# A two-layer attention and mixture-of-experts kernel: who evicts the projections of the first attention, and where three small steps stand in its order

## The chip, the cores and the metric

The kernel runs on one core of one Trainium2 chip. The metric is the device time of one execution in microseconds (us), of which the median of several runs is given. Every engine of the core has a queue of its own and works through it in order: TensorE multiplies, VectorE and ScalarE read its results from PSUM, GpSimd works on SBUF alone, and SyncE issues most loads. Inputs are single-precision floats throughout.

## The reference

Two layers, each an attention with a residual and a mixture of experts with a residual. Only the first attention is touched by the change. There the 1024 tokens of each of two batches are normalised twice and serve as keys and values, together with 77 context tokens; the queries are taken from the tokens too:

```python
xn = _layernorm(x, ln1_w, ln1_b)          # here: the context, 77 tokens
latn = _layernorm(latents, ln2_w, ln2_b)  # here: the normalised tokens, 1024
q = latn @ Wq                             # 16 heads of 64
k, v = jnp.split(jnp.concatenate([xn, latn], axis=1) @ Wkv, 2, axis=-1)
weight = softmax(einsum('bhld,bhnd->bhln', q * scale, k * scale))
out = einsum('bhln,bhnd->bhld', weight, v) ... @ Wo
```

After it come a top-2 router with eight experts of width 1024, a second attention on the 77 context tokens, and a second mixture with a causal convolution.

## The kernel before

**Units.** The first attention is cut into 32 units. A unit is a pair of heads (line names: `j` is 0 or 1) and half of the queries, 512 of them, in four tiles of 128; there are 2 batches, 8 pairs and 2 halves. Four units share one group of four heads (`G`), whose weights are loaded together. A unit goes through these steps:

- `score` (L697): for a tile `t` of queries, the scores against 1024 token keys for both heads, into two PSUM tiles `sc` of their own. VectorE takes the negated maximum of each (L707), ScalarE the exponential with that maximum as bias and the sum as a by-product (L708), which gives the probabilities `pa`.
- `context_scores` (L672 to L687): the same for the 77 context keys, for all four tiles at once; `sums_context` (L690) adds these up on VectorE.
- `join` and `combine` (L715 to L735): the two parts of the softmax are brought to one maximum, the factors `f` are worked out on VectorE in small steps, and `pa` is scaled by them: by GpSimd (L731), and in the last unit half by VectorE (L735) and half by ScalarE (L733). `scale_context` (L739) does it for the context part.
- `turn_tile` (L749): TensorE transposes the scaled probabilities, four blocks of 128 keys into one PSUM tile, for head 0 and then head 1; head 0 is evicted to `pT` by ScalarE (L117), head 1 by VectorE (L121). `k0` is 0 or 4, the first or second half of the keys. `turn_context` (L762) does it for the context part, with ScalarE.
- `attend` (L774): the product of `pT` with the values, 9 tiles of keys, into one PSUM tile `po`; its result is evicted to `oT`, and `out_part` (L642, L650) multiplies that by the output weights and lets VectorE add it to the residual.

**Projections.** Queries and keys of a pair come from `qk_part` in five pieces (L627), values of a group from `v_part` in five pieces (L603). Their products, the transposes, the output products and the routing steps all take their PSUM tiles from one pool of three buffers with the tag "t". A new product or transpose can start only when one of the three has been evicted; the scheduler picks which.

**Who evicts.** `evac` (L108 to L123) takes the engine in `to`. Without it a counter `turn` decides: odd calls go to ScalarE, even ones to VectorE. `v_part`, `qk_part`, the context's transposes and the `attend` results are evicted without `to`.

**Order.** Within the attention the order of each engine's queue is the order of the calls (`manual_schedule`). The loop over the units interleaves three of them: in unit `u`, `score` of `u`, `turn_tile` of the unit before (`prev`), and `attend` of `prev` and of the unit before that. Each unit has four turns `t`. A turn first transposes tile `t` of `prev` with `k0` 0, then scores tile `t`, then does the projections that a table `fill[(u, t)]` has for it, then transposes tile `t` with `k0` 4. `plan` spreads the pieces over turns 0, 1, 1, 2, 2 of a unit. In groups of four units this gives: in unit 0 five pieces of queries and keys; in unit 1 four output products; in units 2 and 3 five of queries and keys and five of values. Routing steps of finished tokens and two layer norms are filled in as well, in units 2 to 4 and 18 to 27, and the second attention's context side in units 30 and 31 (`side_context`, `side_keys`, `side_values`). At turn 3 stand `join`, `combine` and `turn_context`.

After the loop the last unit's transposes and `attend` follow, mixed with the output products and the routing of the third block of tokens. Then comes the expert stage, whose weights SyncE's queue loads (L1063, L1068) once the memory of the attention is free.

Of the kernel before, what the change touches and what calls it, by code (L numbers as in the profile page):

```python
# [10 lines left out]
AF = mybir.ActivationFunctionType  # L11
# [6 lines left out]
B, S, D = 2, 1024, 256  # L18
C = 77
# [30 lines left out]
def tile_two_layers(ctx: ExitStack, tc: tile.TileContext, a: dict, out: bass.AP):  # L50
    nc = tc.nc
# [58 lines left out]
    def evac(dst, src, scale=None, to=None):  # L110

        if to is None:
            turn[0] += 1
            to = nc.scalar if turn[0] % 2 else nc.vector
        if to is nc.scalar:
            if scale is None:
                nc.scalar.copy(dst, src)  # L117
            else:
                nc.scalar.activation(dst, src, AF.Copy, scale=scale)
        elif scale is None:  # L120
            nc.vector.tensor_copy(dst, src)  # L121
        else:
            nc.vector.tensor_scalar_mul(dst, src, scale)  # L123
# [73 lines left out]
    bk1 = mat(const, "L1_xattn_bk", [P, 2], "bk1")  # L197
# [242 lines left out]
    def side_context():  # L440
        ctxT = side["ctxT"] = lnp.tile([P, 2, B, C], F32, tag="ctxT", name="ctxT")
        for b in range(B):
            pt = ps_t.tile([P, 512], F32, tag="t", name="pt")
            for c in range(2):
                nc.tensor.transpose(pt[:, c * C : (c + 1) * C], ctx_sb[:, b, c * P : (c + 1) * P], ident[:C, :C])
            evac(ctxT[:, :, b, :], pt[:, : 2 * C].rearrange("p (c s) -> p c s", c=2))

    def side_keys():
        kT = side["kT"] = lnp.tile([P, 2, B * C], F32, tag="kT1", name="kT1")
        ps = ps_t.tile([P, 512], F32, tag="t", name="pk")  # L450
        for c in range(2):
            for ci in range(2):
                nc.tensor.matmul(
                    ps[:, c * B * C : (c + 1) * B * C],
                    w1a["k"][:, ci, c * P : (c + 1) * P],
                    side["ctxT"][:, ci, :, :].rearrange("p b s -> p (b s)"),
                    start=(ci == 0),
                    stop=(ci == 1),
                )
        for c in range(2):  # L460
            nc.scalar.activation(
                kT[:, c, :], ps[:, c * B * C : (c + 1) * B * C], AF.Identity, bias=bk1[:, c : c + 1]
            )

    def side_values():
        v1 = side["v1"] = lnp.tile([C, B, D], F32, tag="ch", name="v1")
# [48 lines left out]
    NG, GC = 4, H0 * DH0 // 4  # L515
    with ExitStack() as st:
# [76 lines left out]
        def v_part(G, k2):  # L593
            b = G // NG
            if k2 == 0:
                v_of[G] = pj.tile([P, NKT, GC], F32, tag="v", name=f"v_{G}")
            v = v_of[G]
            ps = ps_t.tile([P, 512], F32, tag="t", name="pv")
            kts = [kt for kt in (k2, k2 + 1) if kt < NKT]
            for n, kt in enumerate(kts):  # L600
                r = krows(kt)
                for c in range(2):
                    nc.tensor.matmul(  # L603
                        ps[:r, n * GC : (n + 1) * GC],
                        kvT[b][:, c, kt * P : kt * P + r],
                        groups[G]["v"][:, c, :],
                        start=(c == 0),
                        stop=(c == 1),
                    )
            r = krows(k2)  # L610
            evac(v[:r, k2 : k2 + len(kts), :].rearrange("p n f -> p (n f)"), ps[:r, : len(kts) * GC])

        QK = (("q", 0, 512), ("k", 0, 512), ("k", 512, 1024), ("k", 1024, NKEY), ("q", 512, 1024))

        def qk_part(pair, n):
            G, p = pair // 2, pair % 2
            b = G // NG
            if n == 0:
                qk_of[pair] = (
                    pj.tile([P, S], F32, tag="qT", name="qT"),  # L620
                    pj.tile([P, NKEY], F32, tag="kT", name="kT"),
                )
            nm, n0, n1 = QK[n]
            dst = qk_of[pair][nm == "k"]
            ps = ps_t.tile([P, 512], F32, tag="t", name="pqk")
            for c in range(2):
                nc.tensor.matmul(  # L627
                    ps[:, : n1 - n0],
                    groups[G][nm][:, c, p * P : (p + 1) * P],
                    kvT[b][:, c, n0:n1],  # L630
                    start=(c == 0),
                    stop=(c == 1),
                )
            evac(dst[:, n0:n1], ps[:, : n1 - n0], scale=0.125 if nm == "q" else None)

        def out_part(G, t2):
            b = G // NG
# [51 lines left out]
        def sums_context(U):  # L689
            nc.vector.tensor_reduce(U.l[:, 1, :], U.pB.rearrange("p j t s -> p (j t) s"), AX.X, ALU.add)  # L690
# [28 lines left out]
        def combine(U, last=False):  # L719

            m = U.m
            nc.vector.tensor_tensor(U.l, U.l, U.f, ALU.mult)
            nc.vector.tensor_tensor(m, U.l[:, 0, :], U.l[:, 1, :], ALU.add)
            nc.vector.reciprocal(m, m)
            nc.vector.tensor_tensor(U.f, U.f, m.unsqueeze(1).to_broadcast([P, 2, 8]), ALU.mult)
            for t in range(4):
                for j in range(2):
                    r = 4 * j + t
                    pa, f = U.pa[t][:, j, :], U.f[:, 0, r : r + 1]
                    if not last:  # L730
                        nc.gpsimd.tensor_scalar_mul(pa, pa, f)  # L731
                    elif j:
                        nc.scalar.activation(pa, pa, AF.Copy, scale=f)  # L733
                    else:
                        nc.vector.tensor_scalar_mul(pa, pa, f)  # L735
# [5 lines left out]
        def turn_tile(U, t, k0):  # L741

            if t == 0 and k0 == 0:
                U.pT = [ptp.tile([P, NKT, 512], F32, tag=f"pT{j}", name=f"pT{j}") for j in range(2)]
            for j in range(2):
                ps = ps_t.tile([P, 512], F32, tag="t", name="ptr")
                for n in range(4):
                    kt = k0 + n
                    nc.tensor.transpose(  # L749
                        ps[:, n * P : (n + 1) * P], U.pa[t][:, j, kt * P : (kt + 1) * P], ident  # L750
                    )
                evac(
                    U.pT[j][:, k0 : k0 + 4, t * P : (t + 1) * P],
                    ps.rearrange("p (n q) -> p n q", n=4),
                    to=(nc.scalar, nc.vector)[j],
                )

        def turn_context(U):
# [27 lines left out]
        NPAIR, NU = 2 * B * NG, 4 * B * NG  # L786
        routes = [route(blk) for blk in range(NBLK)]
        with tc.manual_schedule(engines=ORDERED):
# [14 lines left out]
            c = contexts()  # L803
# [27 lines left out]
            for n in range(2):  # L831
                m, s, v, t = latents(2 + n)
# [4 lines left out]
                r = routes[n]  # L837
                u = 18 + n
# [18 lines left out]
            prev = None  # L857
            for u in range(NU):
                U = begin(u)
                if u % 4 == 0 and u // 4 + 1 < B * NG:  # L860
                    groups[u // 4 + 1] = load_group(u // 4 + 1)
                for t in range(4):
                    if prev is not None and t > 0:
                        turn_tile(prev, t, 0)
                    score(U, t)
                    if prev is None and t == 0:
                        context_scores(U)
                    if prev is not None:
                        if t == 0:
                            context_scores(U)  # L870
                            if prev.before is not None:
                                attend(prev.before, range(3, NKT))
                                prev.before = None
                            turn_tile(prev, t, 0)
                            turn_tile(prev, t, 4)
                            scale_context(prev)
                        if t == 3:
                            attend(prev, range(3))
                    if t == 1:
                        sums_context(U)  # L880
                    if t == 3:
                        join(U)
                        for it in late.pop(u, []):
                            it()
                        combine(U, u == NU - 1)
                        if prev is not None:
                            turn_context(prev)
                    for it in fill.pop((u, t), []):
                        it()
                    if prev is not None and t > 0:  # L890
                        turn_tile(prev, t, 4)
                U.before = prev
                prev = U
            assert not late and not fill, (late, fill)


            r, G = routes[2], B * NG - 1
            attend(prev.before, range(3, NKT))
            out_part(G, 0)
            out_part(G, 2)  # L900
# [77 lines left out]
    with ExitStack() as st:  # L978
# [211 lines left out]
        with tc.manual_schedule(engines=ORDERED | {mybir.EngineType.SP}):  # L1190
# [27 lines left out]
            for t in range(NT // B):  # L1218
                n = NB + 2 + t
# [21 lines left out]
            prev = None  # L1241
            for s in range(NSLOT):
# [9 lines left out]
                prev = s, hT  # L1252
# [461 lines left out]
```

## Time and profile before

| what | us |
|---|---|
| median of 3 runs (lowest, highest) | 1760.76 (1760.3, 1763.87) |
| the profiled execution's own time | 1763.98 |
| its span from the first to the last instruction | 1762.3 |
| TensorE busy in the span | 1646.0 |
| VectorE, ScalarE, GpSimd busy | 1027.2, 723.7, 905.9 |
| attention loop, about | 27 to 1165 |
| expert stage, about | 1195 to 1505 |

The page is of one execution. Its engines are PE (TensorE matmul), PEld (TensorE weight load, beside it), DVE (VectorE), ACT (ScalarE), POOL (GpSimd) and SP (SyncE). A row of the timeline has the start in us from the span's start, the duration, the engine, the line, the operation, the tiles as out<-in with partitions x elements, and in brackets how long the engine was idle before it and whose work ended that. A PE row counts two instructions for a product in single precision and one for a transpose. The three evictions that the change is about look like this by shape: a PSUM tile of 128x512 takes ScalarE 587 ns and VectorE 690 ns.

### The profile page before, as it was taken

How to read it: one execution, taken by the hardware profiler on the slowest of the kernel's cores; microseconds unless marked ns; L12 is line 12 of the kernel's file. 1: busy time of each engine (PE TensorE's matmuls, PEld its weight loads, DVE VectorE, ACT ScalarE, POOL GpSimd, SP SyncE). 2: the span in 40 equal slices, each digit the busy share in tenths (PEclk: the TensorE clock that was granted, in tenths of full speed). 3: DMA queues.
4: the chain of work that ended last, by engine and by line, in shares of the span. 5: the costliest groups of instructions: out<-in, count | busy, mean ns of one | idle time of the engine just before them, and what ended most of it. 6: DMA issues, size and time to landing. Idle time of an engine off the chain costs nothing.

```text
span 1762.3 us, 24645 instructions
## 1 busy us (share of the span) xinstructions
PE 1646.0 (93%) x9170; PEld 1044.5 (59%) x9170; DVE 1027.2 (58%) x2052; ACT 723.7 (41%) x1422; POOL 905.9 (51%) x578
## 2 busy tenths in 40 slices
PE   6899999999999999999999999888999999788997
PEld 3455555555555455555555555447899999455564
DVE  4566656565666666776666666553422362676577
ACT  2444444444544444444544454431212233566321
POOL 1567655775676577766777567604030230252425
PEclk9899999999999999999999999999999999898999
DMA  3011211211211210000000000036989998100000
GB/s 115 18 48 66 72 65 68 72 66 67 72 61 66 78 66 7 7 30 13 13 13 7 1 1 4 1 126 242 318 273 314 342 336 281 45 25 1 1 25 24
DMA packets 124860, 151.91 MB, mean 86 GB/s; under 512 B 13211, under 2 KB 112709, under 8 KB 124741
## 3 DMA queue, kind: packets, MB, share of 16 engines
q1 hardware_dynamic: 79984, 102.18, 17.3%
q10 hardware_dynamic: 41685, 39.77, 6.5%
q0 software_dynamic: 3072, 8.39, 1.4%
q8 instruction: 73, 1.20, 0.3%
q14 instruction: 46, 0.38, 0.1%
HBM read 105.10 MB, written 45.22 MB: 85 GB/s over the span
## 4 chain that ended last, share of the span: by engine, by line
PE 65%; DVE 13%; ACT 10%; POOL 6%; issue 2%; DMA 2%; ACTq 1%; another core or an unknown queue 1%; SPq 0%; POOLq 0%; DVEq 0%
PE sc L697 13%; PE ptr L749 10%; PE po L774 8%; PE ph L1091 7%; ACT pa L708 7%; PE po L1111 7%; POOL pa L731 6%; DVE nm L707 5%; PE pqk L627 5%; PE py L642 3%; PE pg L1525 3%; PE pv L603 2%; ACT pT L117 1%; PE sb L672 1%; PE po L1541 1%
## 5 line engine op out<-in xcount | busy, mean ns | idle before, releaser
L731 POOL TENSOR_SCALAR pa<-pa,f 128x1024 f32<-128x1024 f32 x248 | 707.5, 2871 | 362.7 <-ACT pT L117 313.9
L708 ACT ACTIVATE pa<-sc,nm 128x1024 f32<-128x1024 f32 x256 | 283.1, 1110 | 424.0 <-DVE nm L707 416.2
L707 DVE TENSOR_REDUCE nm<-sc 128x1 f32<-128x1024 f32 x256 | 301.5, 1219 | 155.8 <-PE sc L697 155.8
L749 PE MATMUL ptr<-ident,pa 128*128 128x128 f32 x2048 | 285.4, 280 | 53.4 <-DVE pT L121 12.5
L749 PEld LDWEIGHTS ptr<-ident,pa 128*128 128x128 f32 x2048 | 228.0, 142 | 130.7 <-issue 65.3
L774 PE MATMUL po<-pT,v 128*64 128x512 f32 (+1 forms) x1152 | 265.8, 603 | 0.7 <-DVE pT L121 0.7
L121 DVE COPY pT<-ptr 128x512 f32<-128x512 f32 x256 | 175.6, 690 | 154.4 <-PE ptr L749 154.2
L697 PE MATMUL sc<-kT,qT 64*128 64x512 f32 x1024 | 261.6, 627 | 2.6 <-ACT pa L708 2.5
L117 ACT COPY pT<-ptr 128x512 f32<-128x512 f32 (+1 forms) x320 | 180.3, 587 | 118.2 <-PE ptr L749 115.5
L774 PEld LDWEIGHTS po<-pT,v 128*64 128x64 f32 (+1 forms) x1152 | 78.4, 138 | 158.7 <-issue 154.3
L1091 PE MATMUL ph<-xT,w 128*128 128x128 f32 x1248 | 147.1, 276 | 5.7 <-issue 2.8
L1091 PEld LDWEIGHTS ph<-xT,w 128*128 128x128 f32 x1248 | 144.3, 192 | 8.9 <-issue 5.4
L697 PEld LDWEIGHTS sc<-kT,qT 64*128 64x128 f32 x1024 | 89.8, 188 | 89.0 <-issue 83.3
L1111 PE MATMUL po<-w,hT 128*128 128x256 f32 x624 | 141.0, 379 | 0.0
L1111 PEld LDWEIGHTS po<-w,hT 128*128 128x128 f32 x624 | 115.6, 190 | 14.1
L1104 DVE TENSOR_SCALAR hT<-ph,bs 128x128 f32<-128x128 f32 x156 | 43.9, 344 | 123.1 <-PE ph L1091 109.0
L148 POOL TENSOR_TENSOR rstd<-ve,neghalf 128x4 f32<-128x4 f32 (+2 forms) x33 | 26.4, 805 | 157.4 <-DVE ve L141 134.8
L1102 ACT ACTIVATE hT<-ph,bs 128x128 f32<-128x128 f32 x156 | 44.6, 368 | 134.8 <-PE ph L1091 120.7
L935 POOL DMA_INDIRECT yt<-tab_y,pos x32 | 31.3, 978 | 100.1 <-DMA tab_y<-y 91.8
L627 PE MATMUL pqk<-kvT,wk 128*128 128x512 f32 (+1 forms) x192 | 73.1, 510 | 0.0
L603 PE MATMUL pv<-wv,kvT 128*128 128x256 f32 (+1 forms) x288 | 69.9, 383 | 0.6 <-PE pqk L627 0.6
L627 PE MATMUL pqk<-kvT,wq 128*128 128x512 f32 x128 | 66.3, 642 | 3.0 <-DVE pT L121 1.8
(264 smaller groups left out, 1797.0 us busy)
## 6 DMA issues: line engine op xcount, KB each, us to landing
w<-in_L_ffn_W_dram SPq DMA_DIRECT2D x78, 1024.0 KB
tab_x<-zero ACTq DMA_DIRECT2D x32, 512.0 KB
tab_y<-zero ACTq DMA_DIRECT2D x32, 512.0 KB
xs<-tab_x SPq DMA_DIRECT2D x39, 128.0 KB
tab_y<-y ACTq DMA_DIRECT2D x39, 128.0 KB
xr<-in_x_dram SPq DMA_DIRECT2D x4, 512.0 KB
wq<-in_L_xattn_Wq_dram SPq DMA_DIRECT2D x8, 256.0 KB
wk<-in_L_xattn_Wkv_dram SPq DMA_DIRECT2D x8, 256.0 KB
```

The costliest lines, as they stand in the source:

```text
L117: nc.scalar.copy(dst, src)
L121: nc.vector.tensor_copy(dst, src)
L603: nc.tensor.matmul(ps[:r, n * GC : (n + 1) * GC], kvT[b][:, c, kt * P : kt * P + r], groups[G]["v"][:, c, :], start=(c == 0), stop=(c == 1),)
L627: nc.tensor.matmul(ps[:, : n1 - n0], groups[G][nm][:, c, p * P : (p + 1) * P], kvT[b][:, c, n0:n1], start=(c == 0), stop=(c == 1),)
L697: nc.tensor.matmul(sc[j][:, n * 512 : (n + 1) * 512], U.qT[j * DH0 : (j + 1) * DH0, q0 : q0 + P], U.kT[j * DH0 : (j + 1) * DH0, n * 512 : ...
L707: nc.vector.tensor_reduce(U.nm[:, 0, r : r + 1], sc[j], AX.X, ALU.max, negate=True)
L708: nc.scalar.activation(U.pa[t][:, j, :], sc[j], AF.Exp, bias=U.nm[:, 0, r : r + 1], accum_out=U.l[:, 0, r : r + 1])
L731: nc.gpsimd.tensor_scalar_mul(pa, pa, f)
L749: nc.tensor.transpose(ps[:, n * P : (n + 1) * P], U.pa[t][:, j, kt * P : (kt + 1) * P], ident)
L774: nc.tensor.matmul(U.po[j * DH0 : (j + 1) * DH0, :], v[:r, kt, h0 : h0 + DH0], U.pT[j][:r, kt, :], start=(kt == 0), stop=(kt == NKT - 1),)
L1091: nc.tensor.matmul(ps[:, n * TB : (n + 1) * TB], w1[:, c, f * P : (f + 1) * P], xT[:, c, :], start=(c == 0), stop=(c == 1),)
L1111: nc.tensor.matmul(ps[:, :D], hT[:, f, :], w2[:, f, :], start=(f == 0), stop=(f == NF - 1))
```

## The change

Five edits. The evictions of the values, queries, keys and of the context's transposes get `to=nc.vector`, and the bias of the second attention's keys (L461), an activation of ScalarE until now, is added by VectorE. In `turn_tile`, for `k0` 4 in turns 1 and 2, head 0 is evicted by VectorE and head 1 by ScalarE, the other way round than elsewhere. `sums_context` moves in turn 1 from before the fills to after the transposes with `k0` 4. `combine` of the last unit leaves the loop and is called ahead of the `attend` that follows the loop. Since fewer calls of `evac` go by the counter, those that still do (the `attend` results, routing) may fall to the other engine than before.

```diff
@@ side_context
-            evac(ctxT[:, :, b, :], pt[:, : 2 * C].rearrange("p (c s) -> p c s", c=2))
+            evac(ctxT[:, :, b, :], pt[:, : 2 * C].rearrange("p (c s) -> p c s", c=2), to=nc.vector)
@@ side_keys
         for c in range(2):
-            nc.scalar.activation(
-                kT[:, c, :], ps[:, c * B * C : (c + 1) * B * C], AF.Identity, bias=bk1[:, c : c + 1]
-            )
+            nc.vector.tensor_scalar_add(kT[:, c, :], ps[:, c * B * C : (c + 1) * B * C], bk1[:, c : c + 1])
@@ v_part
-            evac(v[:r, k2 : k2 + len(kts), :].rearrange("p n f -> p (n f)"), ps[:r, : len(kts) * GC])
+            evac(v[:r, k2 : k2 + len(kts), :].rearrange("p n f -> p (n f)"), ps[:r, : len(kts) * GC], to=nc.vector)
@@ qk_part
-            evac(dst[:, n0:n1], ps[:, : n1 - n0], scale=0.125 if nm == "q" else None)
+            evac(dst[:, n0:n1], ps[:, : n1 - n0], scale=0.125 if nm == "q" else None, to=nc.vector)
@@ turn_tile
-                    to=(nc.scalar, nc.vector)[j],
+                    to=(nc.scalar, nc.vector)[j if k0 == 0 or t in (0, 3) else 1 - j],
@@ the loop over the units
-                    if t == 1:
-                        sums_context(U)
                     if t == 3:
                         join(U)
                         for it in late.pop(u, []):
                             it()
-                        combine(U, u == NU - 1)
+                        if u < NU - 1:
+                            combine(U)
                         if prev is not None:
                             turn_context(prev)
                     for it in fill.pop((u, t), []):
                         it()
                     if prev is not None and t > 0:
                         turn_tile(prev, t, 4)
+                    if t == 1:
+                        sums_context(U)
@@ after the loop
             r, G = routes[2], B * NG - 1
+            combine(prev, last=True)
             attend(prev.before, range(3, NKT))
```

## The prediction

> **What bounds the kernel now.** I read the page first, then a table of windows by stage, then who TensorE waits for in the attention loop, then single turns in the timeline, last the loop's end. In the table each engine's busy time stands in order after the window's length.
>
> ```profile
> core 0: us, PE busy (x) PEld busy (x) DVE busy (x) ACT busy (x) POOL busy (x), PEclk, DMA share, GB/s
> ...
> 66.00:1110.00 1044.00, 1001.34 (x5434) 562.60 (x5434) 659.54 (x1071) 488.24 (x897) 694.77 (x272) 0.99 0.12 41
> ```
>
> The layer-0 attention is TensorE's: 96% busy, VectorE 63%, ScalarE 47%. So evictions matter only where TensorE waits for one. What it and its weight loads waited for, at the turns of the probabilities (line 749, same window):
>
> ```profile
> its engine sat idle before it (us, times) until:
> ...
>   POOL pa L731: 17.1, 27
>   ACT kT L117: 12.1, 19
>   DVE pT L121: 9.8, 16
> ```
>
> These waits are for one of the three PSUM buffers of tag "t" (GpSimd's scaling apart). Turn 1 of unit 16 shows how they arise:
>
> ```profile
> 596.84 1.99 PE L697 MATMUL sc<-kT,qT 64*128 64x512 f32 x8
> ...
> 598.86 2.36 DVE L707 TENSOR_REDUCE nm<-sc 128x1 f32<-128x1024 f32 x2 [1.22 <-PE sc L697]
> ...
> 601.13 0.78 DVE L690 TENSOR_REDUCE l<-pB 128x8 f32<-128x616 f32 x1
> ...
> 601.28 1.11 ACT L708 ACTIVATE pa<-sc,nm 128x1024 f32<-128x1024 f32 x1
> ...
> 602.37 0.58 ACT L117 COPY kT<-pqk 128x512 f32<-128x512 f32 x1
> 602.50 0.69 DVE L121 COPY kT<-pqk 128x512 f32<-128x512 f32 x1 [0.58 <-PE pqk L627]
> ...
> 603.70 0.69 DVE L121 COPY pT<-ptr 128x512 f32<-128x512 f32 x1 [0.51 <-PE ptr L749]
> ...
> 604.54 0.63 PE L749 MATMUL ptr<-ident,pa 128*128 128x128 f32 x4 [0.44 <-DVE pT L121]
> 605.10 1.99 PE L697 MATMUL sc<-kT,qT 64*128 64x512 f32 x8
> ```
>
> Call the score's start S. VectorE has done both maxima at S+4.3; ScalarE needs them for its two exponentials and is free at S+5.5. The key chunk whose product was done at about S+3.8 therefore leaves PSUM on ScalarE only at S+6.1; the transpose that wants its buffer waits, and a later one again. The next score starts at S+8.26; without waits it would at S+7.3 (score 1.9, two products 3.4, four groups of transposes 2.0). At the end of the loop:
>
> ```profile
> 1149.71 2.74 DVE L735 TENSOR_SCALAR pa<-pa,f 128x1024 f32<-128x1024 f32 x4
> 1149.77 4.27 ACT L733 ACTIVATE pa<-pa,f 128x1024 f32<-128x1024 f32 x4 [0.95 <-DVE f L725]
> 1153.94 1.52 ACT L117 COPY pT<-ptr 77x512 f32<-77x512 f32 x3
> 1154.56 1.12 PE L749 MATMUL ptr<-ident,pa 128*128 128x128 f32 x4 [5.30 <-ACT pT L117]
> 1155.61 7.37 PE L774 MATMUL po<-pT,v 128*64 128x512 f32 x24
> ```
>
> The last unit's scaling stands ahead of the evictions that the unit before still needs; TensorE sits 5.30 us.
>
> **The last scaling.** Nothing is removed, it moves behind those evictions. In other units the transposes of line 762 are followed 2.2 us later by the next work (616.96 to 619.16); here they start at 1147.73, so attend could start at 1149.93 instead of 1155.61: 5.7 us. The same 24 matmuls took 5.37 us at 586.80 and 7.37 here, with a granted clock of 0.73 between 1155.61 and 1163.00. [...] I take the rows: 7.7. The scaling's new cover is attend itself: last turn evicted by VectorE at 1150.7, four small steps of some 0.2 us, factors at 1151.6, four times 1.13 us on ScalarE to 1155.9 (VectorE, 2.74 us, is done before). Queued behind it on ScalarE is the eviction of attend's result (by the count of alternating evictions the 37th, odd, so ScalarE's), ending at 1156.5. Attend waits some 0.5 us for that last turn and ends at 1155.8. The output product starts at 1156.6 instead of 1163.66: **7.0 us**. It has no DMA. SP's first expert weight waits for the scaling and then for a transpose until 1172.06; the latter moves along, so the queue loses nothing. Were the cover gone, 4.3 us would come back.
>
> **Projections on VectorE.** By the groups, ScalarE evicts 18 full value tiles, 16 queries and 15 full key tiles (586 to 597 ns), 5 short values, 8 short keys and three context steps. On VectorE the 49 full ones take 688 ns, 33.7 us, with the short ones 39. VectorE goes from 659.5 to some 698 of 1044 us: no bound. [...] But what decides is the start: S+4.3 against S+5.5. The two swapped tiles and the later context sum (783 ns) belong to the same answer, so I cost them together. With the swap the order after the score is: VectorE maxima, first product, second product, first turn (0.69 each); ScalarE exponentials, second turn. Turn with two long products: second product done at S+5.66, VectorE to 6.35, first turn to 7.04, 0.14 to TensorE, 0.56 for the last transposes: next score at S+7.74. With a short and a long product: 4.3, short key to 4.6, long to 5.29, turn to 5.98: S+6.68. With a query and a one-tile value: S+6.80. Against the score-to-score distances in the timeline (units 8 to 19, by place in the group of four units):
>
> Unit 0, turn 1: 8.26, 7.92, 8.26, then 7.74; turn 2: 7.22, 7.27, 7.22, then 6.68.
> Unit 1, turn 1 (output products, VectorE's already): 7.50, then 7.74 because the turn now follows them; turn 2: 6.27, unchanged.
> Unit 2, turns 1 and 2: 8.26, 8.25, 7.93, 7.93, 7.63, 7.63, then 7.74.
> Unit 3, turn 1: 7.37, 7.89, 7.30, then 6.68; turn 2: 7.11, 7.37, then 6.80 (7.92 in unit 19 holds routing; counted at nothing).
>
> That is 2.9, 2.7 and 1.2 us for the three groups: 6.8. Turns 0 and 3 are at nothing: in turn 3 no projection is evicted, in turn 0 VectorE is idle before the product ends (0.49 us at 596.07); a missing cover there costs 0.7 a turn.
>
> Units 1 to 7 by the same counting give 2.7; 1.0 of loss in unit 4 is in it, where VectorE's layer norm (4 times 0.7 us) leaves no room. Units 20 to 29 lose 2.2: in 20, 21 and 24 VectorE is busy with chains of small routing steps (743.48 to 748.9 in unit 20); the additional eviction of 0.69 and the sum of 0.78, which now stands ahead of the next maxima, delay these, and the exponentials and the next evictions are queued behind them. I took 1.0, 1.0 and 0.6; bounds nothing and 1.5 each. The context side's two evictions in unit 30 end at S+4.9 instead of S+5.8 on ScalarE; TensorE's 2.51 us wait there shrinks by 1.9; the keys give 0.7, the later sum in unit 31 0.6: 3.2. Sum of the loop: 6.8 + 2.7 - 2.2 + 3.2 = 10.5, taken as **10**.
>
> What the trace cannot show is which free buffer the scheduler gives to a transpose. Before, some turns waited for the second turn's buffer though the first's was free earlier (unit 16: 603.52 free, 604.40 taken). After, both end within 0.2 us (7.04, 7.24), so the choice matters less; if none costs, the loop gives 20, if every choice is as bad as before, nothing, or a loss of 3.
>
> **Sum.** 7 + 10 = 17 us. The profiled execution took 1763.98 (span 1762.3 and 1.7 around it), so 1747 for it; the median of the runs lies 3.2 lower: 1760.76 - 17 = 1744. The stages after are TensorE's too (293.64 of 300 us from 1200 to 1500), and their weight loads are issued as its buffers come free, so I let the gain through whole.
>
> **Rivals.**
> 1. Only the end gains (0.20): VectorE's in-order queue gives back in the loop what the earlier start wins. For it: turns that were well chosen are at 7.44 to 7.63 already (units 18, 22), under my 7.74. Against: 12 us of waits for a key on ScalarE. 1754, between 1750 and 1757.
> 2. More (0.17): all choices right and routing turns hidden, 20 from the loop: 1734.
> 3. Slower (0.04): VectorE becomes the turn's bound. Place: turns 1 and 2, 58 of them; price: one eviction more in series, 0.69 each; 40 us against the 17 gained, 1784. It decides from 0.3 us a turn. Against: VectorE has 37% idle.
> 4. The gain does not arrive (0.04): the expert stage's loads (DMA share over 1.0 from 1220 to 1260) set the pace and take up the shift: 1760. Against: TensorE waits 1.1 us for weights in that stage.
>
> The likeliest case, 1738 to 1749, has 0.55. Faster: 0.55, 0.17 and nearly all of the first rival. About 0.2% (3.5 us) is what a measurement of this kernel tells from no change. The range reaches to 1732 and 1754, so that little of rivals 1 and 2 is left out.
>
> **What would show it.** The end: no 5 us gap before the last transposes, granted clock 1.00, 24 matmuls in about 5.4 to 5.9 us, scaling beside them. The loop: "ACT kT", "ACT qT" and "ACT v" gone from TensorE's waits; two-product turns near 7.74, short ones near 6.7; turns with routing longer by up to 1. I am wrong if maxima (line 707) start late after the moved sum in ordinary turns, or if the transposes' wait for VectorE's evictions grows by more than ScalarE's part falls.

## The result and the profile after

| | us |
|---|---|
| before, median of 6 runs (lowest, highest) | 1762.72 (1760.3, 1768.08) |
| after, median of 6 runs (lowest, highest) | 1735.63 (1732.65, 1738.11) |
| after : before | 0.9843, 95% interval 0.9825 to 0.9861 |
| the profiled execution after, its span | 1736.09, 1734.4 |

The change gains 27 us where 17 were forecast. The time lies in the range (1732 to 1754), in its lower third, but outside the band that I held likeliest (1738 to 1749) and next to rival 2's 1734; the loop gave almost twice what I had worked out.

Positions in the two traces say where it came from. The first score starts 0.4 us later than before, the last one 18.5 earlier, the first output product after the loop 26.2 earlier, the first expert product 25.8 and the end 27.9. So the loop gave 18.9 (from first to last score), its end 7.3 to 7.7, and the rest of the kernel 2. I leave that 2 unattributed, because the expert stage with what follows took 567.5 us in the profile of before and 564.5 in a second profile of the same code. It also differs between chips (557.8 with unchanged code in the first experiment), and the medians of the kernel before differ with it, from 1753.72 to 1762.72. The experiments are therefore compared by ratio to the kernel before on the same chip, and by the length of the loop.

The table of windows, for the loop after the change (columns as before: window, its length, PE, PEld, DVE, ACT, POOL busy, granted clock, DMA share, GB/s):

```profile
core 0: us, PE busy (x) PEld busy (x) DVE busy (x) ACT busy (x) POOL busy (x), PEclk, DMA share, GB/s
66.00:1084.00 1018.00, 994.94 (x5397) 557.57 (x5398) 675.81 (x1116) 458.73 (x834) 686.40 (x270) 0.99 0.12 42
```

TensorE is busy for 98% of it (96% before). VectorE has 16 us more busy time in 26 us less and still stands idle for a third. What the transposes' weight loads and products waited for, in the view of their line in this window:

```profile
its engine sat idle before it (us, times) until:
...
  POOL pa L729: 16.9, 32
  ACT pT L117: 12.6, 37
  DVE xr L648: 5.7, 6
  DVE pT L121: 2.1, 1
  DVE kT L121: 1.5, 6
  DVE v L121: 1.3, 2
```

"ACT kT" (12.1), "ACT v" (3.8) and "ACT qT" (3.6) are gone, and "DVE pT" fell from 9.8 to 2.1, while the waits for keys and values on VectorE come to 2.8, less than the 5.8 for keys alone before. "ACT pT", the turns that ScalarE still evicts, rose from 9.5 to 12.6; GpSimd's scaling stays as it was. A turn with a short and a long product, turn 1 of unit 15, in the timeline:

```profile
551.44 1.99 PE L695 MATMUL sc<-kT,qT 64*128 64x512 f32 x8
...
553.46 2.35 DVE L705 TENSOR_REDUCE nm<-sc 128x1 f32<-128x1024 f32 x2 [1.22 <-PE sc L695]
...
555.73 0.23 DVE L121 COPY kT<-pqk 128x77 f32<-128x77 f32 x1
...
555.87 0.68 DVE L121 COPY v<-pv 128x512 f32<-128x512 f32 x1
555.88 1.11 ACT L706 ACTIVATE pa<-sc,nm 128x1024 f32<-128x1024 f32 x1
556.47 0.68 DVE L121 COPY pT<-ptr 128x512 f32<-128x512 f32 x1
...
556.97 1.07 ACT L117 COPY pT<-ptr 128x512 f32<-128x512 f32 x2
557.07 0.78 DVE L688 TENSOR_REDUCE l<-pB 128x8 f32<-128x616 f32 x1
...
557.85 1.99 PE L695 MATMUL sc<-kT,qT 64*128 64x512 f32 x8
```

The order is the forecast one: maxima, both projections, first transpose of the turn on VectorE; exponentials, second transpose on ScalarE; the moved sum (L688) after them, where nobody waits. But the starts say more than the durations: each eviction is listed with 0.68 us, and the next starts 0.60 after it, or 0.14 after the short one that is listed with 0.23. The turn takes 6.41 us; I had added up 6.68.

The loop's end:

```profile
1129.23 1.10 PE L760 MATMUL ptr<-ident,pB 128*77 128x128 f32 x8
...
1130.16 1.33 PE L747 MATMUL ptr<-ident,pa 128*128 128x128 f32 x8
...
1131.42 5.37 PE L772 MATMUL po<-pT,v 128*64 128x512 f32 x24
...
1132.99 2.74 DVE L733 TENSOR_SCALAR pa<-pa,f 128x1024 f32<-128x1024 f32 x4
1133.05 4.27 ACT L731 ACTIVATE pa<-pa,f 128x1024 f32<-128x1024 f32 x4 [1.30 <-DVE f L723]
...
1137.23 0.56 ACT L117 COPY oT<-po 128x512 f32<-128x512 f32 x1
1137.84 1.35 PE L640 MATMUL py<-wo,oT 128*128 128x256 f32 x5 [0.41 <-ACT oT L117]
```

No gap of 5 us, the 24 instructions of `attend` (12 products) in 5.37, the scaling beside them, and behind it on ScalarE the eviction of `oT`, for which TensorE waits 0.41 us.

### The profile page after: what moved, and what is told of

The parts are those of the page before. It is cut to its first block, busy times and chain, and to the rows that moved or that the text cites. A ratio compares the mean times of both kernels' runs of the same rounds, so it can differ in the third digit from the quotient of the medians.

```text
span 1734.4 us, 24678 instructions
## 1 busy us (share of the span) xinstructions
PE 1641.6 (95%) x9170; PEld 1042.8 (60%) x9170; DVE 1055.1 (61%) x2115; ACT 694.6 (40%) x1359; POOL 906.0 (52%) x578
## 4 chain that ended last, share of the span: by engine, by line
PE 70%; DVE 11%; ACT 8%; POOL 7%; DMA 2%; issue 2%; another core or an unknown queue 1%; ACTq 0%; SPq 0%; POOLq 0%; DVEq 0%
PE sc L695 12%; PE ptr L747 11%; PE po L772 7%; PE ph L1091 7%; PE po L1111 7%; PE pqk L625 7%; POOL pa L729 7%; ACT pa L706 4%; DVE nm L705 4%; PE pg L1525 3%; PE pv L601 3%; PE py L640 3%; ACT pT L117 1%; PE po L1541 1%; DMA xs<-tab_x 1%
```

## The experiments

**Theory.** VectorE's maxima end 1.2 us ahead of ScalarE's exponentials, so a projection that VectorE evicts leaves PSUM earlier; that is the loop's gain. The swap and the later sum are worth nothing in sum. The end is a gain of its own, part of it TensorE's clock. **Rivals**: it is the price of an eviction that counts (ScalarE's is lower, 587 against 690 ns, so the gain comes from swap and sum); the three edits in the loop need each other; the end's slow products had waited for evictions, not for the clock.

The length of the loop is from the start of the first score to that of the last; beside it stand the regular stretch, units 8 to 17, and how many windows of 3.41 us at half clock (below: slow windows) the loop had after unit 1. One such window costs 0.9 to 1.7 us (units 3, 4, 20 and 30 of the same code with and without it); they are the subject of experiments 8 to 10.

| kernel | ratio to before (95%) | loop | units 8 to 17 | windows |
|---|---|---|---|---|
| before (as first profiled) | 1 | 1115.7 | 347.7 | 5 |
| end alone | 0.9956 (0.9944 to 0.9969) | 1114.7 | 347.7 | 4 |
| all but the end | 0.9881 (0.9864 to 0.9898) | 1096.8 | 338.9 | 3 |
| no swap | 0.9859 (0.9840 to 0.9879) | 1097.3 | 339.5 | 3 |
| sums early | 0.9855 (0.9834 to 0.9876) | 1097.0 | 340.3 | 1 |
| projections on ScalarE | 0.9970 (0.9959 to 0.9981) | 1117.6 | 346.1 | 4 |
| projections alone | 0.9896 (0.9882 to 0.9910) | 1097.5 | 340.8 | 3 |
| turn by turn | 0.9805 (0.9792 to 0.9818) | 1089.4 | 337.2 | 3 |
| after (as first profiled) | 0.9843 (0.9825 to 0.9861) | 1096.9 | 338.9 | 3 |
| after, again | 0.9843 (0.9830 to 0.9857) | 1096.1 | 338.9 | 3 |
| idle products at the end | 0.9991 (0.9977 to 1.0006) | 1115.0 | 347.7 | 3 |
| before, again (one run) | | 1114.8 | 347.7 | 4 |

**1. The end alone.** Before, with only the last `combine` moved:

```diff
-                        combine(U, u == NU - 1)
+                        if u < NU - 1:
+                            combine(U)
...
+            combine(prev, last=True)
             attend(prev.before, range(3, NKT))
```

> Of the change this kernel has only the last unit's scaling placed after the loop. Theory (the end is worth 7 to 7.7 us by itself): about 1755, a ratio of 0.9957; the turns of the loop keep their lengths to 0.1 us, the 24 matmuls behind the last transposes take 5.4 us at a granted clock of 1.00 instead of 7.37. Rival (the later scaling only pays with the other edits, since its eviction queue is then shorter): within 0.1% of the kernel before, because the output product after it waits longer for ScalarE.

1746.99 against 1755.15, the time of before on the chip of experiments 1 to 4. The last score starts 0.25 us earlier than in before's trace, the first output product 7.9: 7.7 at the end, as expected, with the 24 instructions in 5.37 us at a clock of 1.00. The loop's regular turns are unchanged; that it is 1.0 us shorter is mostly a slow window fewer (unit 4, 1.5 us), less a longer unit 1 (0.7).

**2. All but the end.** After, with these lines put back.

> The whole change without the moved last scaling. Theory (loop and end add up; the loop gave 18.5 us by the distance of the first and last score): about 1743, a ratio of 0.989, with the 5 us gap and the half clock at the end as before. Rival (the loop's gain comes from dips of TensorE's clock that happened to fall differently, and moves with the phase): 3 us or more away from that, with other turns at half clock than in the changed kernel.

1733.6. Loop 18.9 shorter, the end as before, with its half-clock stretch (6.83 us from 1134.99). The two parts add up: 0.9956 times 0.9881 is 0.9838, and the whole measured 0.9843.

**3. No swap.** After, with the evictions of the turns as before:

```diff
-                    to=(nc.scalar, nc.vector)[j if k0 == 0 or t in (0, 3) else 1 - j],
+                    to=(nc.scalar, nc.vector)[j],
```

> The changed kernel with head 0 evicted by ScalarE and head 1 by VectorE in every turn, as before. Theory (what ends a turn is the earlier of the two turn evictions): turns with two long products get shorter, 7.44 instead of 7.66, since ScalarE takes the first turn at S+6.2 while VectorE still evicts the product; turns with a short and a long product get longer, 6.7 instead of 6.42, with a query and one value tile 6.85 instead of 6.63. Per four units the sum is near nothing: 1735, within 2 us. Rival (the swap carries the loop's gain): 5 us slower or more, 1741 and up.

1730.27. Turns with two long products took 7.50 (7.66 with the swap), with a short and a long one 6.66 (6.42), with a query and a one-tile value 7.11 (6.63; 6.85 was expected). The swap costs where the products are long and pays where they are short; over units 8 to 17 that is 0.6 us in its favour, in the whole loop 0.4 to 1.2.

**4. Sums early.** After, with `sums_context` back ahead of the fills.

> The changed kernel with the context sum back ahead of the projections in turn 1. Theory (it delays VectorE's first eviction by 0.78 us): turn 1 of the fourth unit in each group about 7.1 instead of 6.42, of the others 0.1 longer; units 3 and 19 to 21, where VectorE works through chains, shorter by up to 0.8; together about 4 us slower, 1740. Rival (VectorE has room, the place of the sum is worth nothing): 1736 within 1.5 us, and turn 1 of the fourth units unchanged.

1728.71. Turn 1 of every fourth unit (7, 11, 15) went from 6.42 to 7.12 as expected, the other turns 1 not at all. But the whole loop was no longer: 1097.0. It had two half-clock windows fewer than after, in units 3 and 21, 1.7 us each; without them it would have been 3.6 us longer, about as expected. Within that, units 3, 4 and 20 gained 1.3, 0.7 and 0.7 us by the early sum (against after's second profile, which has no slow window in them): there the late sum does stand in front of the maxima, as the prediction feared, and in the short turns it pays. In the time of the kernel the loss did not show. In unit 3 the turn with the stall ahead of after's slow window (2.07 us, until 144.61) had itself become shorter (turn 1 takes 7.26 instead of 8.51 us), though after's second profile has no slow window there with 8.51 either; why unit 21 had one window instead of two stays open.

**5. Projections on ScalarE.** After, but values, queries and keys on ScalarE alone:

```diff
-... ps[:r, : len(kts) * GC], to=nc.vector)
+... ps[:r, : len(kts) * GC], to=nc.scalar)
...
-... scale=0.125 if nm == "q" else None, to=nc.vector)
+... scale=0.125 if nm == "q" else None, to=nc.scalar)
```

> The changed kernel, but all projections (values, queries, keys) are evicted by ScalarE alone instead of VectorE alone. Theory (what counts is when an engine is free: VectorE has its maxima done 4.3 us after the score's start, ScalarE its exponentials only after 5.5): turns with two long products about 7.9 us instead of 7.66, short ones 7.0 to 7.3 instead of 6.42 and 6.63; the loop 10 to 15 us longer than in the changed kernel, ratio to the kernel before about 0.991 to 0.993. Rival (what counts is the cost of one eviction: 587 ns on ScalarE, 690 on VectorE): every such turn 0.1 to 0.2 us shorter, the loop 5 us shorter than in the changed kernel, ratio about 0.982.

1749.77 against 1753.72 of before and 1725.13 of after on this chip. The loop is 21.4 us longer than after's in the same batch and longer than before's. Long turns 7.74, short ones 7.27 and 7.64: the theory's direction and about its turn lengths, but more in sum than the 10 to 15 I had put down, since units 19 to 28, with their routing, lost 10.8 alone (units 8 to 17: 7.2). The same turn as above, of unit 15, here:

```profile
562.99 1.11 ACT L706 ACTIVATE pa<-sc,nm 128x1024 f32<-128x1024 f32 x1 [3.84 <-DVE nm L705]
...
564.10 1.10 ACT L706 ACTIVATE pa<-sc,nm 128x1024 f32<-128x1024 f32 x1
...
565.18 0.22 ACT L117 COPY kT<-pqk 128x77 f32<-128x77 f32 x1
565.29 0.60 ACT L117 COPY v<-pv 128x512 f32<-128x512 f32 x1
565.46 1.53 PE L747 MATMUL ptr<-ident,pa 128*128 128x128 f32 x12 [1.01 <-ACT kT L117]
```

The score started at 559.65. The eviction of the short key starts 5.53 us after that, against 4.29 on VectorE, and TensorE stands 1.01 us for it. Over the window 66 to 1110 the transposes' waits for "ACT kT" come to 33.7 us, where before had 12.1 and the changed kernel none. That ScalarE is 0.1 us quicker at each copy (0.60 for the value here, 0.68 on VectorE) buys nothing.

**6. Projections alone.** Before, with `to=nc.vector` for projections and context and the keys' bias on VectorE; no swap, sums and end as before.

> The kernel before with the projections, the context turns and the keys' bias on VectorE alone; turn evictions not swapped, context sums and last scaling where they were. Theory (the evictions' engine is the cause, swap and sums are worth nothing in sum): the last score 17 to 19 us earlier than before, the end's 7 to 8 us not gained, ratio about 0.989 to 0.990; turns with two long products 7.5, with a short and a long one at turn 1 about 7.2 (the sum stands ahead there). Rival (the three edits need each other): last score less than 12 us earlier, ratio 0.993 or more.

1736.08, 0.9896. Turns with two long products took 7.50 as expected, turn 1 of the fourth units 7.36 (7.2 expected). Its loop is 17.6 us shorter than the mean of the four profiles with before's loop (1115.1); after's two are 18.6 shorter in the mean. With the same number of slow windows swap and sums together are worth 0.6 to 1.3 us. One edit carries the loop's gain.

**7. Turn by turn.** After, with swap and late sum only where the turns above were the shorter for it:

```diff
+        SWAP = {(u, t) for u in (7, 11, 15, 23, 30) for t in (1, 2)}
+        SWAP |= {(u, 2) for u in (4, 8, 12, 16, 28)} | {(u, 1) for u in (3, 26, 27)}
+        LATE = (7, 11, 15, 19, 23, 26, 27, 30)
...
-                    to=(nc.scalar, nc.vector)[j if k0 == 0 or t in (0, 3) else 1 - j],
+                    to=(nc.scalar, nc.vector)[1 - j if k0 == 4 and (u, t) in SWAP else j],
...
+                    if t == 1 and u not in LATE:
+                        sums_context(U)
...
-                    if t == 1:
+                    if t == 1 and u in LATE:
                         sums_context(U)
```

> The changed kernel with swapped turn evictions only in turns whose products are short, and the late context sum only in the units where turn 1 is short. Theory (each regular turn takes the shorter of the two times seen): two long products 7.50 instead of 7.66, short ones as in the changed kernel (6.42, 6.63), units 3, 20 and 21 about 1 us each shorter; together 6 to 9 us less than the changed kernel on the same chip, ratio to before about 0.980 to 0.982. Rival (gains of single turns are given back by the neighbours or lost to clock dips that fall elsewhere): within 3 us of the changed kernel.

1719.89 against 1725.13 of after on the same chip: 5.2 us less, a little under the expected 6 to 9; the loop is 6.7 shorter, with as many slow windows. Each regular turn came out at the shorter of its two times (7.50, 6.42, 6.63). It beats both kernels.

**8. After, again.** The changed kernel itself.

> The changed kernel itself once more, beside the others on one chip. Ratio to before 0.984 to 0.985. If the clock's dips come from where a fixed grid of 3.41 us windows happens to fall on a stall of some 2 us, the same code will show other dips than in its first profile: unit 3's turn 2 (9.79 us with a dip) or unit 21 (41.97 with one) differ by up to 1.7 us, and all regular turns stay at 7.66, 6.42 and 6.63. If a dip belongs to the code, all of them come back at the same places.

0.9843, as at first. Regular turns came back within 0.02 us, but unit 3 took 35.33 instead of 37.03 us and unit 30 took 32.71 instead of 31.10.

**9. Idle products.** Before, with eight more score products of the last unit (16 instructions in the trace, which the expectation calls products), whose result nobody reads, ahead of the last `turn_context`:

```diff
+                        if u == NU - 1:
+                            idle_products(U, 2)
                         if prev is not None:
                             turn_context(prev)
```

> The kernel before with 16 additional score products of the last unit, whose result nobody reads, ahead of the last context turn, so that TensorE works on while it otherwise sat for 5.3 us. Clock theory (the 24 products of attend took 7.37 instead of 5.37 us because TensorE's clock had been halved after the stall): they take about 5.4 us, granted clock 1.00 there, and the kernel is 1.5 to 2 us faster though it does more work, ratio about 0.999. Rival (they were slow because they waited for evictions): 7.3 us again and a ratio of 1.000 or more.

1758.64 against 1760.83; the interval reaches over 1, so the time alone doesn't decide. The trace does. The same 24 instructions of `attend`, first in this kernel, then in before (the row of a table of windows):

```profile
1147.72 5.06 PE L717 MATMUL sc<-kT,qT 64*128 64x512 f32 x16
...
1155.14 5.37 PE L787 MATMUL po<-pT,v 128*64 128x512 f32 x24
```

```profile
1155.61:1162.90 7.29, 7.29 (x25) 2.08 (x24) 0.69 (x1) 0.00 (x0) 0.00 (x0) 0.72 0.01 2
```

5.37 after a TensorE that had been kept busy, with a clock of 1.00 (from 1155.14 to 1160.44); 7.3 at 0.72 after one that had stood for 5.30 us. The transposes ahead of them start at the same time in both (1154.55 and 1154.56), so the evictions that they could wait for do not explain it. So the clock's 2.0 us are real. Both traces have the last score at 1143.07 or 1143.08, and the output product starts 2.46 us earlier here: 2.0 by the clock, and 0.5 because the 24 begin sooner, at 1155.14 instead of 1155.61.

**10. Before, again.**

> The kernel before, profiled once more. Theory (half-clock windows fall where the grid happens to meet a stall of about 2 us): its regular turns come back to 0.1 us, while units 4, 20, 21 and 30 differ by up to 1.7 us each, with other dips. Rival (each dip belongs to its place in the code): dips again in units 4, 20, 21, 30 and at the end, all of the same length.

1760.95 in its one run. Regular turns came back within 0.02 us, but unit 3 took 36.84 (35.18 before), unit 4 38.13 (39.65) and unit 30 32.63 (33.78), while unit 20 kept its half-clock stretch and unit 21 too. Turn 2 of unit 4 shows it best. First before, then this run, TensorE alone:

```profile
182.57 0.63 PE L749 MATMUL ptr<-ident,pa 128*128 128x128 f32 x4 [2.20 <-DVE pT L121]
183.13 3.52 PE L697 MATMUL sc<-kT,qT 64*128 64x512 f32 x8
```

```profile
184.93 0.63 PE L749 MATMUL ptr<-ident,pa 128*128 128x128 f32 x4 [2.20 <-DVE pT L121]
185.49 1.99 PE L697 MATMUL sc<-kT,qT 64*128 64x512 f32 x8
```

The same code, the same stall of 2.20 us, and the score after it in 3.52 us at a granted clock of 0.55 in one run, in 1.99 at 1.00 in the other.

## Why the prediction was right, and where it was too small

**What bounds it, and the mechanism: right.** TensorE's waits for ScalarE's projections were the loop's loss, and moving those to the engine that is free first took them away (experiments 5 and 6). The order inside a turn was the one worked out. The choice of buffers, which the trace of before could not show, cost nothing that can be seen: a turn with two long products takes 7.65 or 7.66 us in every unit from 8 to 17, where before had 7.92 to 8.26. The prediction itself says that the loop then gives 20; its sum of turns came to 10.5 all the same, and it does not say where the rest would lie. One size was off without harm: VectorE came to 675.8 us in the loop, not 698.

**The end: 7.0 forecast, 7.7 measured at the output product's start and 7.3 at its end.** The 7.7 named on the way there were 5.7 of standing and the 2.0 between 7.37 and 5.37. The chain held: factors, four scalings, eviction of `oT`, a short wait. The 0.5 us that I let `attend` wait for its last turn were not there. Experiments 1, 2 and 9 show it alone, absent, and its clock part.

**The loop: the failed term, "taken as 10", measured 18.6** (means of four profiles with before's loop and two of after). The ranges below are those of the profiles; where they are wide, slow windows fell differently. In the means the four parts are 8.8, 6.4, 1.2 and 2.1.

| part | forecast | measured |
|---|---|---|
| units 8 to 19 | 6.8 | 8.8 to 8.9 |
| units 1 to 7 | 2.7 | 4.6 to 7.9 |
| units 20 to 29 | -2.2 | 0.4 to 1.5 |
| units 30 and 31 | 3.2 | 0.5 to 3.2 |

- *Regular turns.* I forecast 7.74, 6.68 and 6.80 and measured 7.66, 6.42 and 6.63. I had added evictions by their listed durations, 0.69 each. Back to back they start 0.60 apart, the short one 0.14 ahead of the next instead of 0.23. A turn with one such step came out 0.08 shorter than the sum, one with a short, a long and a turn in series 0.26 (0.09 and twice 0.08 to 0.09). That makes the 2 us of the first row, 1.0 in each of the first two groups of four units; in the third the turns with routing in units 18 and 19 took it back. The listed durations overlap then, 0.68 listed and 0.60 apart; why, no run here shows.
- *Unit 4.* I counted a loss of 1.0 for VectorE's layer norm. It gained 2.2 against the three profiles of before's loop without a slow window there (38.13 to 35.9) and 3.75 against the one that I read (39.65), whose turn 2 had one that I did not look for. The 2.2 are almost all turn 1 (9.77, then 7.82). Before, the layer norm's four steps stood on VectorE ahead of the eviction of the turn that TensorE waited 2.20 us for (the row at 182.57 in experiment 10); after, TensorE does the 16 transposes and the next score without a wait while these steps run (from 180.88). First before, then after:

```profile
178.95 2.88 DVE L158 TENSOR_SCALAR xh<-xr,mv,rstd 128x256 f32<-128x256 f32 x4
```

```profile
180.07 2.43 PE L747 MATMUL ptr<-ident,pa 128*128 128x128 f32 x16
```

- *Units 20 to 29.* The losses in 20, 21 and 24 were put at 2.6. Unit 21 lost 0.7, unit 20 0.1 against the profiles of before's loop that have a slow window there and 1.0 against the one that has none (after's have none), unit 24 gained 0.1. And I had not counted that turns with a short product stand here too: units 23, 26 and 27 gained 1.5, 0.8 and 0.7. That a moved sum stands in the maxima's way was right for unit 20: experiments 4 and 7 have it 0.7 and 1.1 us shorter.
- *Units 30 and 31.* Here the forecast was too high. With a slow window in unit 30 on both sides or on neither they gave 1.6 to 2.1, not 3.2; 1.1 of the 8.10 us of unit 30's turn 1 in the profile that I read was a slow window (7.01 in before's second profile).
- *The clock.* I looked for it at the 5 us stall of the end, for 2.0 us. It followed on stalls of some 2 us in the loop too (2.20 us ahead of the slow window at 183.45 in before, 2.07 ahead of the one at 145.28 in after): before's loop has three to five slow windows in its four profiles, after's three in both, so of the 18.6 some 1 to 2 us may be fewer slow windows.

**The rivals.** Rival 1 (only the end) is refuted by experiment 2, rival 3 (VectorE the bound) by the turns that got shorter with more work on it, rival 4 (swallowed by the loads) by the positions: the lead at the first expert product, 25.8, was still 27.9 at the end. Rival 2 had the number: 27 us, 20 of them from the loop, and 27 measured. The first half of its reason held (no choice of buffer cost anything that can be seen), the second did not: turns with routing in units 20 and 21 lost 0.1 to 1.0 and 0.7 us. What the loop gave beyond 10 came for the most part from the overlapping evictions (2.0), unit 4 (3.2 against the forecast) and the short turns of units 23, 26 and 27 that I had not counted (3.0).

## What to carry to other kernels

When a PSUM buffer is what TensorE waits for, give its eviction to the engine that comes free first in that turn, not to the one with the shorter instruction; read both from one turn of the timeline. Add up a chain on one engine by the distances between starts, not by durations (here 0.60 against 0.68). And before a long turn is put down to work, read its granted clock, and take a second profile of the same code: what moves between two profiles is not the code's.

## What the runs showed of the hardware

These are readings of the traces of this kernel. TensorE's granted clock was 0.50 for 3.41 us at a time (before, from 183.45), for 6.83 (from 1152.83) or, behind the loop, for 10.24 (from 1620.46). The slow windows of before at 183.45, 750.06 and 794.43 start 166 and 13 times 3.413 us apart. In its second profile they do not start at the same times: there one stands at 146.31 and one at 750.46, 177 times 3.413 us apart. The rows have the columns of the table of windows above: busy times, granted clock, DMA share, GB/s. First the window ahead of a slow one and the slow one itself, in unit 4 of before; then the two windows among which the same stall is divided in before's second profile:

```profile
180.04:183.45 3.41, 1.21 (x10) 0.82 (x9) 2.60 (x4) 0.74 (x2) 3.37 (x2) 1.00 0.42 154
183.45:186.86 3.41, 3.41 (x9) 0.98 (x6) 0.67 (x2) 0.00 (x0) 0.00 (x0) 0.50 0.00 0
```

```profile
180.44:183.85 3.41, 2.29 (x15) 1.42 (x13) 3.41 (x6) 2.68 (x5) 3.41 (x2) 1.00 0.35 126
183.85:187.26 3.41, 2.33 (x12) 1.11 (x12) 1.62 (x3) 0.00 (x0) 1.92 (x1) 1.00 0.08 27
```

In before TensorE was busy for 1.21 us of the window ahead, and the next ran at 0.50; in the second profile, where the stall fell into two windows with 2.29 and 2.33 busy, no slow one followed. The busy time of the window ahead alone does not tell one case from the other: 1.60 us at 746.65 in before was followed by 0.50, 1.60 us at 1083.95 in after by 1.00, and behind the loop of before a window from 1637.52 that was busy throughout was followed by 0.50. What decides whether a slow window follows, the runs do not show.
